# Norms and transpositions of x ahead of a data-dependent branch, in a fixed order, and bias rows loaded behind it

## The chip, the cores and the metric

The kernel runs on one core of one Trainium2 chip. A core has a matmul engine (TensorE, "PE" in the profile; its weight loads are "PEld"), VectorE ("DVE"), ScalarE ("ACT"), GpSimd ("POOL") and SyncE ("SP"), which here only issues DMAs. The engines run on their own and wait for each other by semaphores. The metric is the device time of the program in microseconds (us), as a median of several runs.

## The reference

A network of four graph layers over 512 nodes with 512 features. `src` and `dst` hold 16896 edges, sorted by `dst`, and `edge_type_2` gives each edge one of two types:

```python
h = max(layernorm(x), 0);  x = x + L0(h)   # dense attention, masked by the edges, 8 heads, then an MLP
h = max(layernorm(x), 0);  x = x + L1(h)   # two GIN layers: sum over edges, two products, batch norm
h = max(layernorm(x), 0);  x = x + L2(h)   # GCN: edges weighted by 1/sqrt(degree)
h = max(layernorm(x), 0);  x = x + L3(h)   # two relational layers, weights from 30 bases each
# L0, in the main:
q, k, v = h @ Wq + bq, h @ Wk + bk, h @ Wv + bv
scores = where(adj == 0, -1e9, q k^T / 8);  attn = softmax(scores, axis=1)
```

The change lies at the start: in the first layer norm, in what turns the edge lists into matrices of counts, and in the order of q, k and v.

## The kernel before

Everything has 128 rows (partitions), so x, 512 x 512, is four tiles, t = 0 to 3.

**Start.** SyncE loads the edge lists (`idx`) and x; then Wq, Wk and the first tiles of the basis matrices of layer 3 (the stream `bases`). GpSimd writes `lim` (the bounds that go with each chunk of edges), loads two small tables, writes the ramp `it` (an iota, L150) and, as the stream `rows` is made (L181), issues loads of the first four bias rows (L177). VectorE casts the edge lists to f32 (L390), TensorE transposes them (L392), and VectorE writes `key`: target, source and type of each edge, 128 edges to a chunk, 132 chunks.

**First norm.** `moments` (L342, L343) gives mean and variance of one tile of x. `first_norm` (L376) takes the square root on ScalarE (L378), the reciprocal and the scaled mean on VectorE (L379, L380), and writes h with ScalarE (L381). `flip` (L327) transposes one tile of h with four TensorE instructions into a PSUM bank (L331), and ScalarE copies it into `hT` (L335).

**Check for strays and branch.** The edges are sorted, so each chunk holds targets of a narrow range. `look_for_strays` (L406) compares every target with its bounds, reduces over the chunks on VectorE and over the partitions with a one-column matmul on TensorE (L414), and writes the result as `flag` (L418). All engines load the flag into a register (L460) and jump over `count_strays` if it is zero (L461), as it is for this input. Nothing that stands behind the branch in an engine's queue starts before.

**Counting, with the projections in between.** The matrices of edge counts are sums of one-hot products. For each chunk, `rows_of` (L538) makes two tiles: `hd` on VectorE (L543) and `hs`, for 75 of the 132 chunks on ScalarE (L547) and for the others on VectorE (L549). `count` (L552) multiplies the two with one matmul (L556); there are 204 counts in four blocks, which end at counts 49, 101, 153 and 203 (counted from 0), and rows are made up to 7 chunks ahead. When a block ends, `counted` (L559) empties its two PSUM banks with ScalarE and VectorE before the next block's counts can use them.

The projections of q, k and v (L478, L491) are generators that a plan (L698 to L719) advances between the counts: a "p" in the plan's string is half a projection of one tile, two f32 matmuls, which the profile shows as four records; after every second "p" a bias is added while the bank is copied out by ScalarE (L481). "G" is a basis step (L242), "s" and "S" are score blocks of the attention. FIRST is the number of the count behind which the plan begins, and the items are spread evenly from there to the end of the counting. `select` (L275) builds with 23 small VectorE operations the matrices that the basis steps need; it stands behind count 11. From there on all "p" use one PSUM bank.

**What sets the order.** The program is scheduled at build time: instructions that are not pinned may be moved by the scheduler, while those in `on(...)` (also passed as `keep`) stay in the order in which they are written, on their engine. Before the change the counts and rows up to count 10 were not pinned (`loose`), nor were `select`, the transpositions of h and two of the three ScalarE instructions that touch the norm.

**Behind it.** When the counting is over come the attention proper (VectorE), its products, the MLP and layers 1 to 3, mostly TensorE, which the change does not touch.

Of the kernel before, what the change touches and what calls it, by code (L numbers as in the profile page):

```python
# [74 lines left out]
def gnn_kernel(ctx: ExitStack, tc: tile.TileContext, out: bass.AP, a: dict):  # L75
# [102 lines left out]
            return t  # L178
        return load

    rows = Stream([row_load(i) for i in range(len(ROWS))], 4)  # L181

# [92 lines left out]
    def select():  # L275

        qi = rp.tile([P, NQ], I32, name="qi")
        nc.gpsimd.iota(qi, pattern=[[1, NQ]], base=0, channel_multiplier=0)
        q4 = rp.tile([P, NQ], F32, name="q4")
        nc.vector.tensor_copy(q4, qi)  # L280
        nb = FULL
        vi = rp.tile([P, nb], I32, name="vi")
        nc.gpsimd.iota(vi, pattern=[[-NQ, nb]], base=0, channel_multiplier=1)
        v = rp.tile([P, nb], F32, name="v")
        nc.vector.tensor_copy(v, vi)
        low = rp.tile([P, nb], F32, name="low")
        nc.vector.tensor_scalar(low, v, 0.0, None, op0=ALU.is_ge)
        sel = rp.tile([P, nb], F32, name="sel")
        nc.vector.scalar_tensor_tensor(sel, v, float(NQ - 1), low, op0=ALU.is_le, op1=ALU.mult)
        block = rp.tile([P, nb], F32, name="block")  # L290
        nc.vector.tensor_mul(block, v, sel)
        mine = rp.tile([P, 1], F32, name="mine")
        nc.vector.tensor_reduce(mine, block, AX.X, ALU.add)
        isq = rp.tile([P, NQ], F32, name="isq")
        nc.vector.tensor_scalar(isq, q4, mine, None, op0=ALU.is_equal)

        def fill(to, name, b0, b1, l, bases):

            at = AT1 + 2 * NB * l
            att = scal[:, at:at + 2 * NB].rearrange("p (x b) -> p x b", b=NB)[:, :, bases:bases + b1 - b0]  # L300
            pick = rp.tile([P, 2, b1 - b0], F32, name="pick" + name)
            nc.vector.tensor_mul(pick, att, sel[:, None, b0:b1].to_broadcast([P, 2, b1 - b0]))
            got = rp.tile([P, 2], F32, name="got" + name)
            nc.vector.tensor_reduce(got, pick, AX.X, ALU.add)
            for r in range(2):
                nc.vector.tensor_scalar(to[:, NQ * r:NQ * r + NQ], isq, got[:, r:r + 1], None, op0=ALU.mult)
# [13 lines left out]
    def ts(i):  # L320
        return slice(i * P, (i + 1) * P)

    def on(ins):

        return tc.keep_in_program_order(ins)

    def flip(src, s, dst=None):  # L327

        p = ps()
        for k in range(T):  # L330
            nc.tensor.transpose(p[:, ts(k)], src[:, s, ts(k)], ident)  # L331
# [37 lines left out]


    deg = const.tile([P, T], F32, name="deg")
    mv4 = rp.tile([P, T, 2], F32, name="mv4")
    by4 = rp.tile([P, T, 3], F32, name="by4")
    h = big("A")

    def first_norm(t):  # L376

        nc.scalar.activation(by4[:, t, 0:1], mv4[:, t, 1:2], AF.Sqrt, bias=eps)  # L378
        on(nc.vector.reciprocal(by4[:, t, 1:2], by4[:, t, 0:1]))  # L379
        on(nc.vector.tensor_scalar(by4[:, t, 2:3], mv4[:, t, 0:1], by4[:, t, 1:2], -1.0, op0=ALU.mult, op1=ALU.mult))  # L380
        nc.scalar.activation(h[:, t, :], x[:, t, :], AF.Relu, bias=by4[:, t, 2:3], scale=by4[:, t, 1:2])  # L381

    iot = ep.tile([P, N], F16, name="iot")
# [4 lines left out]
    kn = rp.tile([NCH // 2, 3, 2 * P], F32, name="kn")  # L388
    for i in range(3):
# [12 lines left out]
    stray = ep.tile([P, NCH], F32, name="stray")  # L402
    flag = const.tile([1, 1], I32, name="flag")
# [2 lines left out]
    def look_for_strays():  # L406
        over = rp.tile([P, NCH], F32, name="over")
        on(nc.vector.tensor_tensor(stray, key[:, 0, :], lim[:, 0, :], ALU.is_lt))
        on(nc.vector.tensor_tensor(over, key[:, 0, :], lim[:, 1, :], ALU.is_ge))
        on(nc.vector.tensor_add(stray, stray, over))  # L410
        some = rp.tile([P, 1], F32, name="some")
        on(nc.vector.tensor_reduce(some, stray, AX.X, ALU.max))
        p = ps()
        on(nc.tensor.matmul(p[0:1, 0:1], lhsT=some, rhs=ones, start=True, stop=True))  # L414
        on(nc.vector.tensor_copy(iot, it))
        on(nc.vector.tensor_scalar(key[:, 3, :], key[:, 1, :], -1.0, 0.5, op0=ALU.mult, op1=ALU.add))
        first_norm(2)
        on(nc.vector.tensor_copy(flag, p[0:1, 0:1]))  # L418
# [302 lines left out]
    loose = lambda ins: ins  # L721
# [479 lines left out]
```

## Time and profile before

| | us |
|---|---|
| median of three runs (519.61 to 520.34) | 519.86 |
| the profiled execution | 520.69 |
| its span in the profile | 518.4 |
| TensorE busy | 484.1 (93%) |
| VectorE busy | 399.8 (77%) |
| ScalarE busy | 195.5 (38%) |
| GpSimd busy | 38.1 (7%) |

Times in the profile count from the start of the span. "Busy" counts the time in which an engine executes something; a wait for a semaphore, and the issue of a DMA, are not busy time. In the timeline a row is: start, duration, engine, line of the code, operation, what is written and read, shape, "x" and how many instructions were merged, and in square brackets the idle time ahead of it and what ended that. Rows of one engine may overlap a little, since an engine starts an instruction before the last one's result is written. The chain of waits is the sequence of work that ended last, followed back from the last instruction. In the view by windows each engine has its busy time with the number of instructions in brackets, and behind them stand TensorE's granted clock (as a share of full), the share of busy DMA engines and GB/s.

### The profile page before, as it was taken

How to read it: one execution, taken by the hardware profiler on the slowest of the kernel's cores; microseconds unless marked ns; L12 is line 12 of the kernel's file. 1: busy time of each engine (PE TensorE's matmuls, PEld its weight loads, DVE VectorE, ACT ScalarE, POOL GpSimd, SP SyncE). 2: the span in 40 equal slices, each digit the busy share in tenths (PEclk: the TensorE clock that was granted, in tenths of full speed). 3: DMA queues.
4: the chain of work that ended last, by engine and by line, in shares of the span. 5: the costliest groups of instructions: out<-in, count | busy, mean ns of one | idle time of the engine just before them, and what ended most of it. 6: DMA issues, size and time to landing. Idle time of an engine off the chain costs nothing.

```text
span 518.4 us, 5734 instructions
## 1 busy us (share of the span) xinstructions
PE 484.1 (93%) x2014; PEld 248.6 (48%) x2014; DVE 399.8 (77%) x747; ACT 195.5 (38%) x318; POOL 38.1 (7%) x81
## 2 busy tenths in 40 slices
PE   2999999899998999999999994999799999999996
PEld 2333333345554538864545441644464484446642
DVE  6847587789999689999776982698549999998611
ACT  4876788625345113223321242124623610123000
POOL 7000000000000110300310000000010000000000
PEclk9999999999999999999999998999999999999999
DMA  7999778988968399495323759657972965520011
GB/s 250 272 242 259 175 191 192 248 223 187 224 161 188 92 242 297 169 270 215 117 107 131 184 152 292 236 135 190 272 181 88 316 185 207 192 87 3 0 42 40
DMA packets 42807, 94.06 MB, mean 181 GB/s; under 512 B 2097, under 2 KB 2295, under 8 KB 42775
## 3 DMA queue, kind: packets, MB, share of 16 engines
q1 hardware_dynamic: 34682, 68.30, 48.5%
q0 software_dynamic: 5712, 21.07, 13.7%
q10 hardware_dynamic: 2381, 4.26, 2.5%
q8 instruction: 20, 0.33, 0.3%
q14 instruction: 12, 0.10, 0.1%
HBM read 88.38 MB, written 5.24 MB: 181 GB/s over the span
## 4 chain that ended last, share of the span: by engine, by line
PE 65%; DVE 19%; ACT 9%; DMA 2%; issue 1%; ACTq 0%; DVEq 0%
PE pr L318 17%; PE acc L1109 11%; PE pg L318 9%; PE acc L1075 5%; PE ps L478 4%; PE bas L242 3%; DVE sc L642 3%; ACT sc L643 3%; ACT hs L547 3%; DVE sc L660 3%; DVE wrel L266 3%; PE ao L556 2%; PE acc L935 2%; DMA basis<-in_basis 2%; PE acc L318 2%; DVE half L636 2%
## 5 line engine op out<-in xcount | busy, mean ns | idle before, releaser
L266 DVE SCALAR_TENSOR_TENSOR wrel<-basis,scal,wrel 128x1024 f32<-128x1024 f32 x60 | 74.1, 1282 | 0.0
L242 PE MATMUL bas<-basis,wide 120*32 120x512 f32 (+1 forms) x320 | 44.6, 612 | 7.4 <-DMA basis<-in_basis 6.7
L547 ACT ACTIVATE hs<-iot,key 128x512 f16<-128x512 f16 x75 | 48.8, 711 | 4.7 <-PE ao L556 3.9
L543 DVE TENSOR_SCALAR hd<-iot,key 128x32 f16<-128x32 f16 (+1 forms) x132 | 33.3, 295 | 14.6 <-PE ao L556 14.3
L266 DVE SCALAR_TENSOR_TENSOR w<-basis,scal,w 128x1024 f32<-128x1024 f32 x32 | 39.4, 1283 | 0.0
L643 ACT ACTIVATE sc<-sc 128x2048 f32<-128x2048 f32 (+1 forms) x10 | 15.7, 1568 | 35.3 <-DVE sc L642 35.3
L556 PE MATMUL ao<-hs,hd 128*32 128x512 f16 x204 | 25.8, 396 | 2.8 <-ACT hs L547 2.6
L478 PE MATMUL ps<-bigB,w 128*128 128x512 f32 x56 | 27.2, 615 | 0.9 <-ACT bigD L481 0.6
L350 ACT ACTIVATE sd<-mv,eps 128x1 f32<-128x1 f32 x20 | 5.8, 295 | 43.5 <-DVE mv L343 42.4
L318 PE MATMUL pr<-bigE,w 128*128 128x512 f32 x48 | 21.4, 594 | 0.0
L1157 DVE TENSOR_TENSOR u<-acc,x 128x512 f32<-128x512 f32 x4 | 2.8, 692 | 23.5 <-PE acc L1109 23.5
L318 PE MATMUL pr<-bigD,w 128*128 128x256 f32 x88 | 20.2, 380 | 0.0
L549 DVE TENSOR_SCALAR hs<-iot,key 128x512 f16<-128x512 f16 x57 | 19.3, 347 | 0.0
L642 DVE TENSOR_TENSOR sc<-sc,half 128x2048 f32<-128x2048 f32 (+1 forms) x10 | 18.6, 1863 | 0.2
L242 PEld LDWEIGHTS bas<-basis,wide 120*32 120x32 f32 (+1 forms) x320 | 8.7, 109 | 20.9 <-issue 10.6
L660 DVE TENSOR_TENSOR sc<-sc,rec 128x2048 f32<-128x2048 f32 x8 | 18.3, 2285 | 0.0
L627 PE MATMUL psc<-bigC,bigD 64*128 64x256 f32 x128 | 18.1, 402 | 0.0
L318 PEld LDWEIGHTS pr<-bigD,w 128*128 128x128 f32 x88 | 16.6, 190 | 3.0 <-ACT bigE L880 0.8
L318 PE MATMUL pr<-w,bigE 128*128 128x512 f32 x40 | 17.8, 592 | 0.0
L556 PEld LDWEIGHTS <-hd 128*32 128x32 f16 x204 | 6.1, 94 | 23.8 <-issue 15.1
L478 PEld LDWEIGHTS ps<-bigB,w 128*128 128x128 f32 x56 | 9.7, 189 | 14.9 <-issue 11.1
L629 ACT COPY sc<-psc 128x1024 f32<-128x1024 f32 x16 | 15.6, 1006 | 2.6 <-issue 1.6
(314 smaller groups left out, 969.2 us busy)
## 6 DMA issues: line engine op xcount, KB each, us to landing
basis<-in_basis SPq DMA_DIRECT2D x32, 960.0 KB
basis<-in_basis SPq DMA_DIRECT2D x23, 1024.0 KB
basis<-in_basis SPq DMA_DIRECT2D x16, 448.0 KB
summed<-sums ACTq DMA_DIRECT2D x16, 256.0 KB
w<-in_W POOLq DMA_DIRECT2D x4, 1024.0 KB, 5.9
row<-in_rows POOLq DMA_DIRECT2D x12, 256.0 KB, 8.2
wrel<-summed POOLq DMA_DIRECT2D x4, 512.0 KB, 7.8
w<-in_conv_W1T POOLq DMA_DIRECT2D x2, 1024.0 KB, 5.8
```

The lines of the kernel that those rows point to most:

```text
L242: tc.keep_in_program_order(nc.tensor.matmul(sums[0][32 * j:32 * j + 32, :], lhsT=lhsT, rhs=t[:k, j, :], start=(g == 0), stop=(g == STEPS + ...
L266: on(nc.vector.scalar_tensor_tensor(to[r][:, i:i + 2, :], t[:, i:i + 2, :], scal[:, at:at + 1], to[r][:, i:i + 2, :], op0=ALU.mult, op1=AL ...
L318: nc.tensor.matmul(p, lhsT=lhsT, rhs=rhs, start=(i == 0), stop=(i == len(pairs) - 1))
L478: on(nc.tensor.matmul(p, lhsT=w[:, k, ts(m)], rhs=made["hT"][:, k, :], start=(k == 0), stop=(k == T - 1)))
L543: keep(nc.vector.tensor_scalar(hd[:, :w], iot[:, GW * groups_of[c][0]:GW * groups_of[c][0] + w], key[:, 0, c:c + 1], key[:, 2, c:c + 1], o ...
L547: keep(nc.scalar.activation(hs, iot, AF.Sign, bias=key[:, 3, c:c + 1]))
L556: keep(nc.tensor.matmul(cnt[b][GW * (g % T):GW * (g % T) + GW, :], lhsT=hd[:, at:at + GW], rhs=hs, start=(c == in_bank[g][b][0]), stop=(c ...
L642: on(nc.vector.tensor_sub(s, s, half[:, 0:1, :].to_broadcast([P, H // pieces, NH])))
L643: on(nc.scalar.activation(s, s, AF.Exp, scale=HD ** -0.5))
L660: on(nc.vector.tensor_mul(self.sc, self.sc, rec[:, None, :].to_broadcast([P, H, NH])))
L1075: nc.tensor.matmul(self.out[t], lhsT=self.hT[:, k, ts(t)], rhs=self.root[:, k, :], start=(k == 0), stop=False)
L1109: nc.tensor.matmul(self.out[t], lhsT=self.uT[r][:, k, ts(t)], rhs=wrel[r][:, k, :], start=False, stop=(r == 1 and k == T - 1))
```

## The change

Moments, norms and transpositions of all four tiles of x are written ahead of the check for strays, all pinned, with the square root taken out of `first_norm` so that it can stand earlier in ScalarE's order. Before, the moments and norm of tile 3 stood inside `look_for_strays`, behind the flag, tile 2's norm just ahead of it, and all four transpositions behind the branch in the text, though the scheduler put two of them ahead of it. The cast of the ramp (`iot`) moves ahead of the first moments, and the last part of `key` ahead of the check. The stream `rows` starts behind the branch, so the first four bias rows are issued by GpSimd there. `select`, and all rows and counts, are pinned, and FIRST is 4 in place of 9. No arithmetic is added or left out.

```diff
-    rows = Stream([row_load(i) for i in range(len(ROWS))], 4)
+    rows = Stream([row_load(i) for i in range(len(ROWS))], 0)
+    rows.ahead = 4
...
-        nc.vector.tensor_copy(q4, qi)
+        on(nc.vector.tensor_copy(q4, qi))
...
-    def flip(src, s, dst=None):
+    def flip(src, s, dst=None, keep=lambda ins: ins):
 
         p = ps()
         for k in range(T):
-            nc.tensor.transpose(p[:, ts(k)], src[:, s, ts(k)], ident)
+            keep(nc.tensor.transpose(p[:, ts(k)], src[:, s, ts(k)], ident))
...
-        nc.scalar.copy(dst[:, :, ts(s)], p)
+        keep(nc.scalar.copy(dst[:, :, ts(s)], p))
...
+    made = {"hT": big("B")}
...
+    def root(t):
+        on(nc.scalar.activation(by4[:, t, 0:1], mv4[:, t, 1:2], AF.Sqrt, bias=eps))
+
     def first_norm(t):
 
-        nc.scalar.activation(by4[:, t, 0:1], mv4[:, t, 1:2], AF.Sqrt, bias=eps)
         on(nc.vector.reciprocal(by4[:, t, 1:2], by4[:, t, 0:1]))
...
-        nc.scalar.activation(h[:, t, :], x[:, t, :], AF.Relu, bias=by4[:, t, 2:3], scale=by4[:, t, 1:2])
+        on(nc.scalar.activation(h[:, t, :], x[:, t, :], AF.Relu, bias=by4[:, t, 2:3], scale=by4[:, t, 1:2]))
...
+    on(nc.vector.tensor_copy(iot, it))
     moments(mv4[:, 0, :], x[:, 0, :], on)
     on(nc.vector.tensor_copy(key[:, 0:2, :], pk[:, 0:2, :]))
     on(nc.vector.tensor_scalar(key[:, 2, :], pk[:, 2, :], 0.0, LESS, op0=ALU.is_equal, op1=ALU.max))
 
+    root(0)
     moments(mv4[:, 1, :], x[:, 1, :], on)
-    for t in range(2):
-        first_norm(t)
+    first_norm(0)
+    root(1)
     moments(mv4[:, 2, :], x[:, 2, :], on)
+    root(2)
+    first_norm(1)
+    flip(h, 0, made["hT"], on)
+    moments(mv4[:, 3, :], x[:, 3, :], on)
+    root(3)
+    first_norm(2)
+    flip(h, 1, made["hT"], on)
+    first_norm(3)
+    for t in (2, 3):
+        flip(h, t, made["hT"], on)
+    on(nc.vector.tensor_scalar(key[:, 3, :], key[:, 1, :], -1.0, 0.5, op0=ALU.mult, op1=ALU.add))
...
         on(nc.tensor.matmul(p[0:1, 0:1], lhsT=some, rhs=ones, start=True, stop=True))
-        on(nc.vector.tensor_copy(iot, it))
-        on(nc.vector.tensor_scalar(key[:, 3, :], key[:, 1, :], -1.0, 0.5, op0=ALU.mult, op1=ALU.add))
-        first_norm(2)
         on(nc.vector.tensor_copy(flag, p[0:1, 0:1]))
-        moments(mv4[:, 3, :], x[:, 3, :], on)
-        first_norm(3)
...
     bases.start(AHEAD)
 
-    made = {}
-    made["h"], made["hT"] = h, big("B")
-    for t in range(T):
-        flip(made["h"], t, made["hT"])
+    rows.start(4)
+    made["h"] = h
...
-    FIRST = 9
+    FIRST = 4
...
-        keep = on if n > 10 else loose
...
-            rows_of(needed[made_rows], keep)
+            rows_of(needed[made_rows], on)
...
-        count(g, c, cnt, keep)
+        count(g, c, cnt, on)
```

The diff pins the other operations of `select` in the same way as the one shown.

More of the change, by code (lines that the diff above doesn't have):

```diff
@@ L284, in select @@
         v = rp.tile([P, nb], F32, name="v")
-        nc.vector.tensor_copy(v, vi)
+        on(nc.vector.tensor_copy(v, vi))
         low = rp.tile([P, nb], F32, name="low")
-        nc.vector.tensor_scalar(low, v, 0.0, None, op0=ALU.is_ge)
+        on(nc.vector.tensor_scalar(low, v, 0.0, None, op0=ALU.is_ge))
         sel = rp.tile([P, nb], F32, name="sel")
-        nc.vector.scalar_tensor_tensor(sel, v, float(NQ - 1), low, op0=ALU.is_le, op1=ALU.mult)
+        on(nc.vector.scalar_tensor_tensor(sel, v, float(NQ - 1), low, op0=ALU.is_le, op1=ALU.mult))
         block = rp.tile([P, nb], F32, name="block")
-        nc.vector.tensor_mul(block, v, sel)
+        on(nc.vector.tensor_mul(block, v, sel))
         mine = rp.tile([P, 1], F32, name="mine")
-        nc.vector.tensor_reduce(mine, block, AX.X, ALU.add)
+        on(nc.vector.tensor_reduce(mine, block, AX.X, ALU.add))
         isq = rp.tile([P, NQ], F32, name="isq")
-        nc.vector.tensor_scalar(isq, q4, mine, None, op0=ALU.is_equal)
+        on(nc.vector.tensor_scalar(isq, q4, mine, None, op0=ALU.is_equal))
         def fill(to, name, b0, b1, l, bases):
@@ L301, in fill @@
             pick = rp.tile([P, 2, b1 - b0], F32, name="pick" + name)
-            nc.vector.tensor_mul(pick, att, sel[:, None, b0:b1].to_broadcast([P, 2, b1 - b0]))
+            on(nc.vector.tensor_mul(pick, att, sel[:, None, b0:b1].to_broadcast([P, 2, b1 - b0])))
             got = rp.tile([P, 2], F32, name="got" + name)
-            nc.vector.tensor_reduce(got, pick, AX.X, ALU.add)
+            on(nc.vector.tensor_reduce(got, pick, AX.X, ALU.add))
             for r in range(2):
-                nc.vector.tensor_scalar(to[:, NQ * r:NQ * r + NQ], isq, got[:, r:r + 1], None, op0=ALU.mult)
+                on(nc.vector.tensor_scalar(to[:, NQ * r:NQ * r + NQ], isq, got[:, r:r + 1], None, op0=ALU.mult))
         for l in range(2):
@@ L374, in gnn_kernel @@
     h = big("A")
+    def root(t):
+        on(nc.scalar.activation(by4[:, t, 0:1], mv4[:, t, 1:2], AF.Sqrt, bias=eps))
     def first_norm(t):
-        nc.scalar.activation(by4[:, t, 0:1], mv4[:, t, 1:2], AF.Sqrt, bias=eps)
         on(nc.vector.reciprocal(by4[:, t, 1:2], by4[:, t, 0:1]))
         on(nc.vector.tensor_scalar(by4[:, t, 2:3], mv4[:, t, 0:1], by4[:, t, 1:2], -1.0, op0=ALU.mult, op1=ALU.mult))
-        nc.scalar.activation(h[:, t, :], x[:, t, :], AF.Relu, bias=by4[:, t, 2:3], scale=by4[:, t, 1:2])
-    iot = ep.tile([P, N], F16, name="iot")
+        on(nc.scalar.activation(h[:, t, :], x[:, t, :], AF.Relu, bias=by4[:, t, 2:3], scale=by4[:, t, 1:2]))
     key = ep.tile([P, 4, NCH], F32, name="key")
@@ L388, in gnn_kernel @@
     kn = rp.tile([NCH // 2, 3, 2 * P], F32, name="kn")
+    iot = ep.tile([P, N], F16, name="iot")
     for i in range(3):
@@ L719, in gnn_kernel @@
     plan.setdefault(len(order) - 14, []).append(lambda: blocks[0].pairs())
-    loose = lambda ins: ins
     made_rows = 0
     for n, (t, g, c) in enumerate(order):
-        keep = on if n > 10 else loose
         if n == 0 or order[n - 1][0] < t:
```

## The prediction

> **What bounds the kernel now.** I read the page first (TensorE is busy 93% of the span, and only the first of the 40 slices is thin, with 2 tenths), then the chain of waits, then the timeline of the first 35 us engine by engine, then single lines. The chain is unbroken work from 12.36 us on: count matmuls (L556) and projections (L478) on TensorE with ScalarE's rows and copies (L547, L481) in between up to 105 us, VectorE in the attention, TensorE again behind it. Nothing in it starts at a fixed time, and the DMA wait at 310.60 us (10.82 us) begins only when a buffer comes free. So a stage 1 that ends later moves the end by as much. The start of that chain:
>
> ```profile
> 12.49 1.10 PE ps L331 x4
> ...
> 15.58 1.11 PE psc L331 x4
> 16.69 1.15 PE ao L556 x7
> 17.84 2.54 PE psc L478 x4
> 20.37 0.33 PE ao L556 x4
> 20.70 1.91 PE psc L478 x4
> ```
>
> The columns are start and duration. Two of the four transpositions of h (L331) run behind the branch, then counts, and at 17.77 the first half projection ("p" in the plan: two f32 matmuls, four records) begins. It lasts 2.54 us, the next 1.91. The timeline shows what stands before it:
>
> ```profile
> 4.93 0.58 POOL L150 IOTA it<- 128x512 int32 x1
> ...
> 5.29 0.69 DVE L342 BATCH_NORM_STATS2 st<-x 128x6 f32<-128x512 f32 x1 [0.69 <-DMA x<-in_x]
> ...
> 7.87 1.52 ACT L381 ACTIVATE bigA<-x,by 128x512 f32<-128x512 f32 x2
> ...
> 10.94 0.14 DVE L418 CAST flag<-ps 1x1 int32<-1x1 f32 x1
> ...
> 12.44 0.18 DVE L343 BATCH_NORM_AGGREGATE mv<-st 128x2 f32<-128x6 f32 x1 [0.77 <-DVEq L461]
> ```
>
> The flag is ready at 11.08, VectorE goes on at 12.44 and TensorE at 12.46: the register load and branch cost 1.36 us.
>
> **Part 1: the flag comes later.** All four norms and transpositions now stand, in a fixed order, ahead of the flag's matmul (L414), on every engine. Durations and distances are those of the rows. VectorE: the cast of iot now precedes the first moments and needs the iota, done at 5.51; so it runs at 5.55 and the first statistics start at 5.88, not 5.29. Moments take 0.82 (6.63 to 7.45), the two key operations 0.51, the next moments 0.82, reciprocal and scaling 0.38: the first scale is ready at about 8.4. From there ScalarE, in its fixed order, is the limit: h0 8.45 (0.71 to the next), two square roots of 0.30, h1 at 9.91 (it waits 0.15 for its scale), copy of hT 10.62 (0.50), root, h2 11.42, copy 12.13, h3 12.63 to 13.44. TensorE's last four transpositions take 1.10 from 13.49 (8 took 1.97 at 8.73), and only then may the one-column matmul of 0.19 run: the flag is done at about **14.9**, 3.8 us later than now. VectorE's three new moments and the stray comparisons are done by 13.0 and hide beside that. With 1.36 us of branch VectorE starts the row tiles at 16.3. The unknown here is ScalarE's queue; 14.2 if the iota runs earlier, 15.7 if each hand-over costs 0.1 us more.
>
> **Part 2: the restart.** In exchange nothing but counting is left behind the branch. VectorE needs 0.22 us for each hd and 0.27 for each hs (ten hd in 2.21 us, three hs in 0.87); ScalarE's hs takes 0.66. The plan starts at count 4 rather than 9. The fifth count needs the hd of the fourth row, chunk 1: two hd and two hs, then two hd, 17.7, and the first half projection starts at about 17.85 against 17.77: **+0.1**. But only 5 counts are behind it, where the records before 17.77 show 11: 6 counts of 0.107 (5 in 0.54, at 42.30) are still to come, **+0.65**. Moving the start of the plan removes no work.
>
> **Part 3: TensorE's pace after a rest.** The granted-clock column says 1.00 for the first 20 us, but the same transposition tells otherwise:
>
> ```profile
> L331 PE MATMUL pr<-ident,bigA x24: 272/273/273, 247.5 to 461.1; 128*128 128x128 f32 x24
> ...
> L331 PE MATMUL psc<-ident,bigA x12: 421/421/477, 8.7 to 16.3; 128*128 128x128 f32 x12
> ```
>
> It takes 421 ns up to 16.3 us and 273 later, and the first half projection lost 2.54 - 1.91 = 0.63 us. Half pace for the first 1.26 us of it explains this: full pace from about 19.1, 3.5 us after TensorE became busy without a break (15.58). The one other rest is seen with its clock:
>
> ```profile
> 310.00:320.00 10.00, 4.08 (x32) 1.02 (x30) 3.75 (x13) 4.12 (x7) 0.75 (x1) 0.97 0.85 222
> 320.00:325.00 5.00, 3.54 (x14) 1.78 (x15) 0.00 (x0) 0.52 (x1) 0.00 (x0) 0.50 1.04 390
> 325.00:330.00 5.00, 5.00 (x21) 4.03 (x21) 4.88 (x5) 0.66 (x2) 0.00 (x0) 0.87 1.04 386
> ```
>
> (The column after the last "(x..)" is the granted clock.) Work resumed at 321.46, eight basis matmuls took 1.94 us where 0.86 is usual, and 0.87 in the next window means 1.3 us more of half pace: to 326.3, 4.8 us after the restart. So a restart costs 3.5 to 4.8 us of half pace. After the change the transpositions ahead of the branch have gaps (each waits for its h), then TensorE rests from 14.8 to 17.0, and dense work begins at about 17.4: full pace at 20.9 to 22.2. Half of the time since 17.85 is lost, 1.5 to 2.2, less the 0.63 lost now: +0.9 to +1.5, I take **+1.2**. From below: if those transpositions already bring full pace, nothing is lost and the 0.63 is won back.
>
> [...]
>
> **Part 4: select in one piece.** Its 23 small VectorE operations (0.17 to 0.23 each; 18.10 to 22.1 now, with four hs among them, so 2.9 net) are now pinned at count 11: dependent ones are 0.2 apart, 3.7 us in one block from about 22.2 to 25.9. Queued behind it is the hd of chunk 22, which count 21 needs. With that hd done at 26.2 and Part 3's pace, TensorE gets there at about 27 (three half projections and 16 counts after 17.85), so the block is covered: **0**. Without Part 3's loss it gets there at 25.4 and waits 0.8.
>
> **Part 5: the first row end.** At count 49 the next block's counts need the banks that ScalarE and VectorE empty. Now two half projections (3.70 us from 34.67) cover that, and counts resume at 38.38; after, one half projection and a basis step, 1.91 + 0.86 = 2.77, cover a release that takes 2.9 to 3.7: +0.1 to +0.9, less what ScalarE gains by having copied the previous projection earlier; I take **+0.3**, bounds 0 and 0.8. The basis step itself is only moved (from count 57).
>
> **Costed at nothing.** The four bias-row issues on GpSimd (2.15 us) go behind the branch: there they delay the iotas and memsets of select to about 18.7, which VectorE needs at 22.2; uncovered they would cost what exceeds 3.5 us. Their first reader (L494) comes after 69 us. Their absence early lets x land sooner, which gains nothing since the iota ends the first wait. SP's queue passes the branch 3.8 us later, with two basis loads and Wv: the third basis tile is wanted past 54 us and Wv at 67.61, against 13.1 us for the slowest landing of a weight that the DMA view shows in the first 40 us (Wo), and requests already queued keep the DMA engines busy meanwhile (share 1.02 from 10 to 20). Uncovered, at most those 3.8 us. Pinned rows and counts up to count 10 add no instruction.
>
> **Sum:** 0.1 + 0.65 + 1.2 + 0 + 0.3 = **+2.2 us**. The profiled execution took 520.69 us (span 518.4, 2.29 around it), so about 522.9 for it; it lies 0.83 above the median of the three runs, so that I state **522.0** for the median, 519.86 + 2.2 rounded. The forecast's own range: from +0.9 (full pace, 0.63 won back, select's 0.8 showing: 0.1 + 0.65 - 0.63 + 0.8) to +4.0 (flag 0.8 later, 1.5, 0.8): 520.8 to 523.9.
>
> **Rivals.** *No change that can be told:* the transpositions ahead of the branch wake TensorE, and the select block and the row end are covered: 0.1 + 0.65 - 0.63 = +0.1, 520.0. For it: there TensorE is busy some 4.4 of 5.3 us. Against it: now it is busy 3.4 of the 4.2 us from 12.49 to 16.69, partly with counts, and the first projection is slow still.
>
> *Faster:* the hand-back of the one projection bank. Weight loads of L478 wait 1.3 us in all for ScalarE's copies into bigC and 2.1 for those into bigD. If the shifted plan removed all of it, -3.4 + 2.2 = -1.2, 518.7; it decides once more than 3.2 us of those waits go. Against it: the plan leaves 4, 3, 7, 9, 4, 4, 5 counts between a copy and the next projection now, and 4, 4, 3, 7, 4, 4, 8 after; hardly different.
>
> That the order isn't obeyed is unlikely, since all those instructions are pinned.
>
> **How the numbers follow.** Forecast 0.70, no change 0.20, faster 0.10. A measurement can tell 0.2%, 1.04 us, from nothing: faster means under 518.82, slower over 520.90. Nearly all of the forecast lies above it (0.68), with 0.02 falling to "same": 0.10, 0.22, 0.68. The range reaches down past the no-change case to 519.7 and up to 523.7; what is left out is the faster case and the tail of a late flag with a long half pace.
>
> **What would show it.** The flag at 14.2 to 15.7, VectorE's first hd about 1.4 us behind it, the first L478 at 17.4 to 18.6 lasting 3 us or more, select in one block of 3.5 us or more, counts resuming 2.9 us or more after the 50th. Wrong: a first half projection of 1.9 us; a flag before 13; or a shift at 35 us that is gone at 105, which would mean that stage 1 has slack that I don't see.

## The result and the profile after

| us | before | after |
|---|---|---|
| median (range) of four runs each, same chip | 520.10 (519.61 to 522.06) | 528.31 (527.71 to 530.00) |
| profiled execution, its span | 520.69, 518.4 | 530.00, 528.1 |
| TensorE, VectorE, ScalarE busy | 484.1, 399.8, 195.5 | 488.5, 404.2, 195.3 |

After over before is 1.0156, with a 95% interval of 1.0120 to 1.0191: **8.2 us slower** by the medians, where +2.2 was predicted. A second set of runs (e9 below) gave 1.0164 [1.0140, 1.0188]. The sign was right and the size was not.

It arises in stage 1. From the first matmul of the attention's sums (line 654 in before, 664 in after) to the end the two profiles differ by 1.1 us only, and that has a cause of its own (below). The table cuts stage 1 at points that every kernel here has: the flag's end, the starts of the first four half projections (p0 to p3), and that first matmul of the sums. The columns with "to" are distances.

| us | flag | p0 | p0 to p1 | p1 to p2 | p2 to p3 | p3 to sums | sums at |
|---|---|---|---|---|---|---|---|
| before | 11.08 | 17.77 | 2.86 | 2.46 | 2.46 | 75.97 | 101.52 |
| after | 18.23 | 21.46 | 4.63 | 2.45 | 3.26 | 78.31 | 110.11 |
| after less before | +7.15 | +3.69 | +1.77 | 0 | +0.80 | +2.34 | +8.59 |

The prediction's terms for the same cuts were +0.1 (p0), +1.2 (p0 to p1), 0 (p2 to p3) and +0.95 (the counts deferred, 0.65, and the row end, 0.3, both behind p3). Every cut is above its term, the first by most. The timeline of after shows why the flag is late (columns as before: start, duration, engine, line, operation, in brackets the idle time ahead and what ended it):

```profile
2.75 3.45 POOL L144 TENSOR_SCALAR lim<-lim 128x66 f32<-128x66 f32 x3
3.36 2.99 DVE L394 CAST kn<-idx 66x256 f32<-66x256 int32 x3 [2.46 <-DMA idx<-in_dst]
...
6.68 0.58 POOL L150 IOTA it<- 128x512 int32 x1
...
7.29 2.15 DVE L397 CAST iot<-it 128x512 f16<-128x512 int32 x1 [0.94 <-POOL it L150]
7.33 1.82 POOL L471 MEMSET apart<- 128x2048 bf16 x1
9.08 2.15 POOL L177 DMA_DIRECT2D row<-in_rows  x4
...
18.08 0.15 DVE L432 CAST flag<-psc 1x1 int32<-1x1 f32 x1 [1.57 <-PE psc L431]
...
21.46 3.78 PE L488 MATMUL psc<-bigB,w 128*128 128x512 f32 x4
```

The same operations in the timeline of before:

```profile
2.75 1.71 POOL L144 TENSOR_SCALAR lim<-lim 128x66 f32<-128x66 f32 x3
3.26 1.34 DVE L390 CAST kn<-idx 66x256 f32<-66x256 int32 x3 [2.36 <-DMA idx<-in_dst]
...
7.72 1.82 POOL L459 MEMSET apart<- 128x2048 bf16 x1
...
10.09 0.42 DVE L415 CAST iot<-it 128x512 f16<-128x512 int32 x1
```

The cast of `iot` took 0.42 us before, at 10.09, when GpSimd was idle. Here it lies beside GpSimd's memset of `apart`, which keeps its usual 1.82, and takes 2.15, ending 0.29 behind the memset. The three casts of `kn` took 1.34 before and take 2.99 here. The first of them alone, and GpSimd's third addition, from the timeline around 3.8 us:

```profile
3.36 2.51 DVE L394 CAST kn<-idx 66x256 f32<-66x256 int32 x1 [2.46 <-DMA idx<-in_dst]
...
3.46 2.73 POOL L144 TENSOR_SCALAR lim<-lim 128x66 f32<-128x66 f32 x1
```

The cast takes 2.51 us where the two behind it take 0.31 each, and the addition 2.73 where the same one took 0.99 in before. This also pushes GpSimd's iota from 4.93 to 6.68 and so the cast of `iot` behind it. The row at 9.08 says another thing: GpSimd issues the four bias rows there, ahead of the branch, although they are written behind it, since they are not pinned.

The chain of waits of after, start and duration, shows the rest of the loss:

```profile
20.05 1.48 PE ao L566 x5
21.53 3.71 PE psc L488 x4
...
175.98 4.54 PE ps L664 x12
```

and at the same place in the chain of before:

```profile
167.41 2.86 PE ps L654 x12
```

Five counts in 1.48 us and a first half projection of 3.71 (2.54 before): TensorE at half pace. The first record of the granted clock in each trace, full pace, stands at 19.1 us in before and at 26.0 here; ahead of it the clock's column in the view by windows shows 1.00, and the half pace is seen in the durations alone. The 12 matmuls at 175.98 account for what is lost behind stage 1. By the clock's records TensorE is at half pace from 176.2 to 179.6, behind a wait that both kernels have. A timeline row and a window of after (the clock is the third number from the end):

```profile
175.98 1.93 PE L664 MATMUL ps<-z,ident 128*128 128x256 f32 x4 [1.78 <-DVE z L658]
```

```profile
175.00:180.00 5.00, 4.02 (x11) 3.26 (x12) 2.89 (x2) 1.96 (x3) 0.00 (x0) 0.66 0.97 205
```

The profile of e9, the same kernel once more, does not have it (2.86 for the 12).

### The profile page after: what moved, and what is told of

It is laid out like the page before. It is cut to its first block, busy times and chain, and to the rows that moved or that the text cites. A ratio compares the mean times of both kernels' runs of the same rounds, so it can differ in the third digit from the quotient of the medians.

```text
span 528.1 us, 5737 instructions
## 1 busy us (share of the span) xinstructions
PE 488.5 (93%) x2014; PEld 249.8 (47%) x2014; DVE 404.2 (77%) x747; ACT 195.3 (37%) x318; POOL 39.5 (7%) x81
## 4 chain that ended last, share of the span: by engine, by line
PE 63%; DVE 19%; ACT 9%; DMA 3%; issue 2%; ACTq 0%; DVEq 0%
PE pr L319 17%; PE acc L1116 10%; PE pg L319 9%; PE acc L1082 5%; PE ps L488 4%; PE bas L243 3%; DVE sc L652 3%; ACT sc L653 3%; DVE wrel L267 2%; ACT hs L557 2%; PE acc L942 2%; DVE sc L670 2%; DMA basis<-in_basis 2%; PE ao L566 2%; PE acc L319 2%
## 5 line engine op out<-in xcount | busy, mean ns | idle before, releaser
L653 ACT ACTIVATE sc<-sc 128x2048 f32<-128x2048 f32 (+1 forms) x10 | 15.7, 1570 | 35.6 <-DVE sc L652 28.6
L501 PE MATMUL ps<-w,bigB 128*128 128x512 f32 x32 | 15.9, 618 | 1.0 <-DVE bigE L504 1.0
```

Of the source, the lines that this page charges most:

```text
L653: on(nc.scalar.activation(s, s, AF.Exp, scale=HD ** -0.5))
```

## The experiments

The profiled positions of the runs that are compared by them, cut as above. Medians and ratios stand with each run; before had 519.87, 520.58, 520.56 and 520.62 in the four sets (7, 11, 16 and 27 runs).

| us | kn, iot casts | flag | p0 | p0 to p1 | p2 to p3 | p3 to sums | sums at |
|---|---|---|---|---|---|---|---|
| e1 | 3.05, 0.42 | 15.15 | 18.38 | 4.45 | 3.42 | 78.29 | 106.99 |
| e2 | 3.10, 0.44 | 12.00 | 19.42 | 4.68 | 3.19 | 78.29 | 108.05 |
| e3 | 1.26, 2.15 | 16.35 | 19.62 | 4.40 | 2.45 | 78.29 | 107.22 |
| e4 | 4.44, 0.41 | 17.23 | 21.97 | 3.94 | 2.45 | 75.90 | 106.72 |
| e5 | 3.05, 0.42 | 15.13 | 19.95 | 3.48 | 2.46 | 75.90 | 104.24 |
| e6 | 1.21, 0.43 | 14.78 | 18.02 | 3.96 | 3.42 | 78.30 | 106.15 |
| e7 | 2.98, 0.42 | 14.69 | 18.33 | 2.45 | 3.42 | 78.31 | 104.96 |
| e9 | 3.14, 2.15 | 18.23 | 21.46 | 3.61 | 3.42 | 78.30 | 109.25 |
| e13 | 0.89, 0.42 | 14.19 | 17.42 | 4.00 | 3.42 | 78.29 | 105.58 |
| e14 | 1.05, 0.42 | 13.64 | 18.46 | 4.48 | 2.46 | 75.90 | 103.76 |
| e15 | 1.28, 0.42 | 10.65 | 17.34 | (p0 to p2 5.57) | 2.45 | 78.29 | 103.65 |
| e16 | 1.27, 0.42 | 11.06 | 17.75 | 3.66 | 2.46 | 75.96 | 102.28 |

Two columns take only two values each. p3 to sums is 78.3 in every kernel whose plan begins at count 4 and 75.9 to 76.0 in every one that begins at count 9. p2 to p3 is 3.2 to 3.4 only where that plan, the pinned `select` and the pinned first rows and counts are together.

### First set: one part of the change taken back

**e1, the cast of `iot` back ahead of the flag's copy**

```diff
-    on(nc.vector.tensor_copy(iot, it))
     moments(mv4[:, 0, :], x[:, 0, :], on)
...
+        on(nc.vector.tensor_copy(iot, it))
         on(nc.vector.tensor_copy(flag, p[0:1, 0:1]))
```

> After the change, with the cast of iot moved back behind the reduction of the strays; all else stays. Theory A (the flag is late, and of its 7.1 us some 3.3 come from two VectorE casts that GpSimd's work beside them stretches: kn 0.86 to 2.51, iot 0.42 to 2.15): the cast's wait of 0.6 and its stretch of 1.7 leave the path to the flag, which comes at 14.3 to 16.0; 2.3 us less than the changed kernel, about 526. Rival B (what was lost lies behind the branch, in the plan that starts at count 4 and in the pinned counts; the flag's delay is covered): less than 0.5 us of change.

525.99, ratio 1.0109 [1.0088, 1.0131]. The flag comes 3.08 us earlier than in after, the time falls by 2.3.

**e2, norms and transpositions as before; rows, `select` and plan as changed**

```diff
-    for t in (2, 3):
-        flip(h, t, made["hT"], on)
...
+    made["h"], made["hT"] = h, big("B")
+    for t in range(T):
+        flip(made["h"], t, made["hT"])
```

> After the change, with the block of moments, norms and transpositions as it was before the change (tiles 2 and 3 around the flag, two transpositions behind the branch, iot and the last part of key inside the check); select, rows and counts stay pinned and the plan begins at count 4. Theory A: the flag comes at 11 to 12.7 and 5 to 7.5 us are won back, 521 to 523. Rival B: within 1.5 us of the changed kernel, 527 or more.

526.59, ratio 1.0106 [1.0074, 1.0137]. The flag is back at 12.00, and yet p0 starts at 19.42: with the rows pinned behind the transpositions' copies in ScalarE's order, the first `hs` starts at 17.52 where before it started at 14.10. Undoing the largest suspect alone gains 1.7 us, between the two times expected, because the pinned queue takes over what the flag no longer costs.

**e3, `select` not pinned**

```diff
-        on(nc.vector.tensor_copy(q4, qi))
+        nc.vector.tensor_copy(q4, qi)
```

> After the change, with select's 23 VectorE operations not pinned. Theory A: the count that waits 0.4 us for VectorE's hd at 31.48 and the pinned block in front of it cost 0.8, so 527.5. Rival C (the block is covered by TensorE's half pace, as predicted): no change, 528.3. Rival B says nothing of it.

526.15, ratio 1.0105 [1.0056, 1.0154]. p2 to p3 falls from 3.26 to 2.45, with no wait of a count for VectorE. In this profile the flag is also 1.88 earlier, since the casts of `kn` were not stretched.

**e4, the plan at count 9 and the first counts not pinned**

```diff
-    FIRST = 4
+    FIRST = 9
...
+        keep = on if n > 10 else loose
-            rows_of(needed[made_rows], on)
+            rows_of(needed[made_rows], keep)
```

> After the change, with FIRST back at 9 and rows and counts up to count 10 not pinned. Theory A: 0 to 1 us less (the row end at count 49 is covered by two half projections again), 527.3 to 528.3. Rival B: 4 us less or more, 524 or under.

525.83, ratio 1.0102 [1.0075, 1.0128]. p3 to sums is 75.90, as before. All four are 1.0% over the kernel before, and no single part explains the 1.6%.

### Second set: parts alone, and the two suspects of the start

**e5, norms and transpositions alone** (e1, e3 and e4 together)

> The kernel before with the norms and transpositions of all of x ahead of the flag alone: iot is cast late, select is not pinned, rows and counts are as before with the plan from count 9 (the bias rows stay where the change puts them). Theory A2 (three costs that partly stand in for each other: the late flag, the pinned queue behind the branch, select in one block): the part that I predicted, without the stretched casts and the block, is left; flag at 14.3 to 16, 1.5 to 3 us over the kernel before, 521.5 to 523. Rival D (pinning costs most, the norm block by itself little): within 1 us of before.

523.03, ratio 1.0051 [1.0035, 1.0068], at the upper end of what was expected.

**e6, after with GpSimd's memset held back until `key` is written**

```diff
-    nc.gpsimd.memset(apart, 1.0)
+    late = rp.tile([1, 1], F32, name="late")
+    on(nc.gpsimd.tensor_copy(late, key[0:1, 0, 0:1]))
+    on(nc.gpsimd.memset(apart, 1.0))
```

> The changed kernel, with GpSimd's memset of apart made to wait for key, so that it can't run beside the cast of iot. The order on VectorE is unchanged. If the cast is stretched by the memset beside it: 0.42 us in place of 2.15, flag 1.7 earlier than in the changed kernel, time 1.7 less, 526.6. If the cast is slow because of its place or of the DMAs that land then: 2.15 still, no change.

524.21, ratio 1.0068 [1.0052, 1.0083]. Rows of its timeline:

```profile
3.39 1.21 DVE L394 CAST kn<-idx 66x256 f32<-66x256 int32 x3 [2.49 <-DMA idx<-in_dst]
...
5.55 0.43 DVE L397 CAST iot<-it 128x512 f16<-128x512 int32 x1 [0.95 <-POOL it L150]
...
7.33 1.79 POOL L473 MEMSET apart<- 128x2048 bf16 x1
...
14.64 0.14 DVE L432 CAST flag<-psc 1x1 int32<-1x1 f32 x1 [1.57 <-PE psc L431]
...
18.02 3.49 PE L490 MATMUL psc<-bigB,w 128*128 128x512 f32 x4
```

VectorE's work and order are those of after. On GpSimd the memset stands behind three of the bias rows' issues, and in this profile the casts of `kn` are not stretched, so that the iota and the cast of `iot` come earlier. The cast takes 0.43 at 5.55 and the flag is there at 14.78: the prediction's 5.55 and 14.9. e3 has unstretched casts of `kn` too, but the memset beside the cast of `iot`:

```profile
3.01 1.26 DVE L394 CAST kn<-idx 66x256 f32<-66x256 int32 x3 [2.11 <-DMA idx<-in_dst]
...
5.41 2.15 DVE L397 CAST iot<-it 128x512 f16<-128x512 int32 x1 [1.13 <-POOL it L150]
5.44 1.82 POOL L471 MEMSET apart<- 128x2048 bf16 x1
```

So the work ahead of the flag was rightly summed; what was missing is what GpSimd does beside it. The time fell by 4.1 us by the medians where 1.7 was expected; the unstretched casts of `kn` would account for much of that, but why they are so here is not known.

**e7, e1 with TensorE kept busy ahead of the branch** (16 matmuls of zeros, whose result is not used)

```diff
+    def wake(n):
+        for _ in range(n):
+            on(nc.tensor.matmul(cnt_first[0], lhsT=zero, rhs=zero[:, 0:1].to_broadcast([P, 512]), start=True, stop=True))
...
         on(nc.tensor.matmul(p[0:1, 0:1], lhsT=some, rhs=ones, start=True, stop=True))
+        wake(14)
```

> The changed kernel with iot cast late, and 16 matmuls on zeros added on TensorE (one behind each of the first two transpositions, 14 behind the flag's matmul), whose result is not used. If TensorE's rest ahead of the counts costs half pace: the first half projection takes 1.9 to 2.6 us in place of 3.7, and the time is 1 to 1.5 less than with iot late alone (525.99), 524.7. If the 3.7 us are a wait for something else: 3.7 still, no gain, up to 0.5 slower.

524.46, ratio 1.0072 [1.0054, 1.0090]. TensorE's rows in its timeline:

```profile
14.44 3.22 PE L398 MATMUL ao<-zero 128*128 128x512 f16 x14
...
18.33 1.98 PE L498 MATMUL psc<-bigB,w 128*128 128x512 f32 x4
...
20.78 1.98 PE L498 MATMUL psc<-bigB,w 128*128 128x512 f32 x4
```

With full pace from 13.0 us p0 takes 1.98, p0 to p1 is 2.45 in place of 4.45, and the sums come 2.03 earlier than in e1 (1.5 by the medians). The slow start is the clock's, not a wait for data.

**e8, before, with GpSimd's additions held back behind the casts of `kn`**

```diff
-    for t in range(1, T):
-        nc.gpsimd.tensor_scalar_add(over_tiles[:, :, t, :], over_tiles[:, :, t, :], float(P * t))
...
+    late = rp.tile([1, 1], F32, name="late")
+    on(nc.gpsimd.tensor_copy(late, kn[0:1, 2, 0:1]))
+    for t in range(1, T):
+        on(nc.gpsimd.tensor_scalar_add(over_tiles[:, :, t, :], over_tiles[:, :, t, :], float(P * t)))
...
-    nc.gpsimd.memset(apart, 1.0)
+    on(nc.gpsimd.memset(apart, 1.0))
```

> The kernel before, with GpSimd's three additions to lim made to wait until the casts of kn are done. Four of six profiles so far show these casts at 3.0 to 4.4 us in all, two at 1.3. If that is work of both engines side by side: 1.3 us always, no run of the kernel near 521.3, and the median 0.5 to 1.5 under before, 518.5 to 519.4. If the casts wait for their DMA: 3.0 or more in some profiles, no change.

524.64, ratio 1.0074 [1.0046, 1.0103], for another reason than the one tried: GpSimd, free of the additions, issued the bias rows at 3.94 instead of 5.59, the third tile of x landed late (VectorE idle 2.90 us at 10.75, ended by the load of x), and the flag came at 13.60. The order of the issues on GpSimd does matter here, in the direction opposite to the change's.

### Third set: a repeat, and attempts at a faster kernel

**e9, after once more**

> The changed kernel once more, beside runs of the kernel before on the same chip. Theory A2: iot's cast is stretched to some 2.1 us again in the profile (the memset of apart always starts beside it) and the time is 3 us or more over e6 (524.2), 527 to 528.5. If the stretch was chance: 0.42 us, 524 to 525.

529.08, ratio 1.0164 [1.0140, 1.0188]. Both casts stretched as in the first profile, 3.14 and 2.15.

**e10, before with additions, `scal` and bias rows all behind the casts of `kn`**

```diff
...
-    rows = Stream([row_load(i) for i in range(len(ROWS))], 4)
+    rows = Stream([row_load(i) for i in range(len(ROWS))], 0)
+    rows.ahead = 4
...
+    on(nc.gpsimd.memset(apart, 1.0))
...
+    rows.start(4)
```

The additions and the load of `scal` move as the additions do in e8.

> The kernel before, with GpSimd's additions to lim behind the casts of kn, the small table scal behind these, and the bias rows behind the memset of apart, so that nothing large is loaded beside x (e8 loaded the rows 1.65 us earlier, and the third tile of x came 2.9 us late). kn 1.2 to 1.3 us in the profile; if the stretch of kn is what spreads the runs of the kernel before (519.6 to 522), all runs lie near its lowest: median 0.5 to 1 less. If not: no change.

520.75, ratio 1.0003 [0.9991, 1.0015]. Casts of 0.69, flag at 11.06: nothing gained, nothing lost.

**e11, before with e7's matmuls of zeros; e12, e10 and e11 together** (the results of those matmuls are not used)

```diff
+    wake(13)
     for t in range(2):
         first_norm(t)
+    for t in range(2):
+        flip(h, t, made["hT"], on)
...
+        wake(6)
```

> The kernel before, with 19 matmuls on zeros on TensorE ahead of the branch (13 behind the edge lists' transpositions, 6 behind the flag's matmul), the first two transpositions pinned. The half pace costs the kernel before at least 0.63 us in the first half projection and some 0.4 in the counts ahead of it: 0.6 to 1.2 us less than before. Rival: TensorE isn't what the first projection waits for, no change.

> Both of the two last in one kernel: 1 to 2 us less than the kernel before if they add up.

524.48, ratio 1.0082 [1.0059, 1.0105], and 525.14, ratio 1.0092 [1.0076, 1.0107]. TensorE in e11:

```profile
10.78 0.60 PE L331 MATMUL ps<-ident,bigA 128*128 128x128 f32 x4
...
15.71 0.63 PE L331 MATMUL ps<-ident,bigA 128*128 128x128 f32 x4 [2.36 <-DVEq L473]
...
19.91 3.78 PE L489 MATMUL psc<-bigB,w 128*128 128x512 f32 x4
```

The transpositions run at twice the pace (four in 0.60, 1.1 before), but the branch still leaves TensorE 2.36 us idle, and the clock falls back to half from 17.6 to 24.4, over p0, which takes 3.78 in place of 2.60. The flag is 1.04 later too, at 12.12. Here the early work did not help, since the pace that it won was lost again behind the branch: of the 3.41 us up to 17.6 TensorE was busy for 1.39. No kernel of the study beats the one before.

### Fourth set: what each part costs with the casts undisturbed

**e13, after with GpSimd's additions, `scal` and memset held back behind the cast of `iot`**

```diff
...
     on(nc.vector.tensor_copy(iot, it))
+    late = rp.tile([1, 1], F16, name="late")
+    on(nc.gpsimd.tensor_copy(late, iot[0:1, 0:1]))
+    for t in range(1, T):
+        on(nc.gpsimd.tensor_scalar_add(over_tiles[:, :, t, :], over_tiles[:, :, t, :], float(P * t)))
+    nc.gpsimd.dma_start(scal, a["scal"].to_broadcast([P, NSC]))
...
-    nc.gpsimd.memset(apart, 1.0)
+    on(nc.gpsimd.memset(apart, 1.0))
```

VectorE's order is that of after, in which the cast of `iot` already stands right behind those of `kn`; it runs earlier because GpSimd, without the additions, has the iota done earlier. The load of `scal` is not pinned and was issued ahead of the additions, at 3.38.

> The changed kernel with GpSimd kept quiet while VectorE makes its casts: the cast of iot moved straight behind the three of kn, and behind it, in this order, GpSimd's three additions on lim, the load of scal and, behind the flag's work, the memset of apart. Nothing is left out. Theory (both stretched casts are paid in nearly every run of the changed kernel): kn's casts 0.7 to 1.3 us and iot's 0.43, the flag at 13.9 to 14.9, and the time is the changed kernel's 529.1 less 1.7 for iot and 1.7 for kn and what hangs on them, 522.3 to 523.5. Rival (the stretch of kn is an accident of single profiles and most runs of the kernel before have it too): as with the memset alone held back, 524.2. Rival (a late flag isn't what the time hangs on): above 526.

524.37, ratio 1.0084 [1.0067, 1.0101]. From its timeline:

```profile
3.15 0.89 DVE L391 CAST kn<-idx 66x256 f32<-66x256 int32 x3 [2.25 <-DMA idx<-in_dst]
...
3.96 0.42 DVE L394 CAST iot<-it 128x512 f16<-128x512 int32 x1
...
4.65 1.09 POOL L398 TENSOR_SCALAR lim<-lim 128x66 f32<-128x66 f32 x3
...
14.04 0.15 DVE L434 CAST flag<-psc 1x1 int32<-1x1 f32 x1 [1.57 <-PE psc L433]
...
17.42 3.54 PE L490 MATMUL psc<-bigB,w 128*128 128x512 f32 x4
...
26.97 0.39 PE L568 MATMUL ao<-hs,hd 128*32 128x512 f16 x1 [0.57 <-DVE hd L555]
```

Neither cast is stretched, and p0 starts at 17.42, earlier than in before. The sums come 4.53 us earlier than in after's profile, and the median is 4.7 below e9's. The expected 522.3 to 523.5 was wrong: the time is e6's (524.2), which was the rival's number. The rival's reason, that most runs of the kernel before have stretched casts of `kn` too, is not shown; e6's profile has unstretched ones, which explains the equal times as well.

**e14, e5 with the casts undisturbed in the way of e10**

> Norms and transpositions ahead of the check alone (iot late, select unpinned, the plan at count 9), with GpSimd's additions, the load of scal and the memset of apart held back behind kn's casts. Theory (kn's stretch is part of what the norm block alone cost in its run, 2.45 us): the flag near 13.5, first half projection near 18.3, 521.0 to 521.8 against 520.6. Rival (the stretch isn't in most runs, and the block costs that by its half pace and ScalarE's queue): 523.0 as before.

521.79, ratio 1.0032 [1.0015, 1.0050]. Between the two expectations, and its interval overlaps e5's [1.0035, 1.0068]: likely part of e5's time was the stretch of `kn`, but this is not shown.

**e15, before with the plan at count 4 alone**

```diff
-    FIRST = 9
+    FIRST = 4
```

> The kernel before with one edit: the plan starts at count 4, not at 9. Theory (the term of 0.65 us for counts deferred, and 1.4 us at the row end of count 153, where the second score block moves behind its counts): the two score blocks of that place 4.4 us apart instead of 3.0, the first half projection within 0.2 us of 17.77, and 522.0 to 522.7 against 520.6. Rival (counts deferred fill waits that stand later in stage 1): 520.6 within 0.5, stage 1 ending within 0.5 us of 101.5.

523.27, ratio 1.0053 [1.0034, 1.0073], a little above what was expected. The start is 0.43 us earlier in this profile, p0 6.69 behind the flag as in before. p0 to p3 is 8.02 against 7.78, p3 to sums 78.29 against 75.97. Of the 2.3 us between these two, 1.4 lie where two score blocks (L621) stand close together. TensorE there in before, then in e15:

```profile
77.83 0.60 PE L621 MATMUL psc<-apart,far_off 128*128 128x512 bf16 x2
...
79.43 0.64 PE L556 MATMUL ao<-hs,hd 128*32 128x512 f16 x6
80.31 0.59 PE L556 MATMUL ao<-hs,hd 128*32 128x512 f16 x2 [0.24 <-ACT hs L547]
80.83 0.61 PE L621 MATMUL psc<-apart,far_off 128*128 128x512 bf16 x2
```

```profile
78.56 0.60 PE L621 MATMUL psc<-apart,far_off 128*128 128x512 bf16 x2
...
81.22 0.39 PE L556 MATMUL ao<-hs,hd 128*32 128x512 f16 x2 [0.45 <-ACT hs L547]
81.83 0.38 PE L556 MATMUL ao<-hs,hd 128*32 128x512 f16 x1 [0.22 <-ACT hs L547]
82.44 0.59 PE L556 MATMUL ao<-hs,hd 128*32 128x512 f16 x2 [0.24 <-ACT hs L547]
82.97 0.60 PE L621 MATMUL psc<-apart,far_off 128*128 128x512 bf16 x2
```

4.41 us from one block to the next in place of 3.00 (4.40 in after and e13). Two more counts stand between them, and counts wait for `hs` three times (0.91 in all) instead of once (0.24). ScalarE, which makes `hs`, is late there: its timeline in e15 shows

```profile
79.50 1.06 ACT L643 ACTIVATE sc<-sc 128x1024 f32<-128x1024 f32 x1 [0.33 <-DVE sc L642]
80.46 1.93 ACT L547 ACTIVATE hs<-iot,key 128x512 f16<-128x512 f16 x3
```

The attention's exponential (L643) waits for VectorE and stands in ScalarE's order ahead of the rows that TensorE needs next.

**e16, before with `select` pinned alone**

> The kernel before with one edit: select's VectorE operations pinned in one block at count 11. Theory (VectorE is close to what TensorE waits for there): the block 3.5 to 4.3 us long, one wait of TensorE for a hd ahead of the third half projection or the fourth, 0.8 to 1.2 us on stage 1, 521.4 to 521.8 against 520.6. Rival (covered, as the prediction had it): no wait, 520.6 within 0.4.

520.81, ratio 1.0005 [0.9991, 1.0018]. The block is 4.16 us long (19.14 to 23.30), and TensorE does not wait for it:

```profile
23.86 1.98 PE L478 MATMUL ps<-bigB,w 128*128 128x512 f32 x4
25.77 0.61 PE L556 MATMUL ao<-hs,hd 128*32 128x512 f16 x6
26.32 1.99 PE L478 MATMUL ps<-bigB,w 128*128 128x512 f32 x4
```

Alone it is covered, as predicted, and the theory of the expectation was wrong.

**The sum.** By the ratios times 520.6, the parts alone cost 1.7 (e14, norms and transpositions), 2.8 (e15, the plan) and 0.3 us (e16, `select`), together 4.7; the three together without stretched casts cost 4.4 [3.5, 5.3] (e13). The change as it is costs 8.5 [7.3, 9.8] (e9). What remains, some 4.1, goes with the two casts: the flags of e9 and e13 are 4.04 apart. The pinning of the first rows and counts was not run alone; in e13 it is included.

## Why the prediction was right in sign and wrong in size

In the profile of after, stage 1 ends some 6.3 us later than the prediction's terms had it. 3.3 of these are the flag, 1.4 lie behind p3, 0.8 are a wait behind `select`, 0.6 the slow start and 0.3 the restart.

**Part 1, the flag: the failed step.** The prediction took the cast of `iot` at its duration of before ("so it runs at 5.55 and the first statistics start at 5.88") and allowed only for an earlier iota and for hand-overs (14.2 to 15.7). It moved the cast from a place where GpSimd was idle to one beside GpSimd's memset. Measured: 2.15 in place of 0.42, and a flag at 18.23. With neither cast stretched (e6) the flag is at 14.78, with that of `iot` alone stretched (e3) at 16.35. So of the 3.45 us from 14.78 to 18.23 the memset beside `iot` costs 1.57. The other 1.88 come with the casts of `kn`, which the change does not touch, by way of GpSimd's addition and iota beside them (the iota at 6.68 in place of 4.93).

That the `iot` stretch is the memset's is shown: it is there in after, e9 and e3 (2.15 each), where the two overlap, and gone wherever they don't (0.41 to 0.44), in e6 at nearly the same time as in e3. For `kn` less is certain. It was 2.98 to 3.14 in six profiles of the changed kernel and its variants, 4.44 in e4 (its third cast alone lasts from 3.90 to 7.40, long past the additions, and ends 0.15 behind the memset of `apart`), but 1.21 to 1.26 in e3 and e6, 1.27 to 1.34 in before, e15 and e16, whose start is the same code, and 1.02 in e11. Additions and casts overlap in all of these. In the six, the first cast ends at 5.86 to 5.88 wherever it had started (3.21 to 3.37). What decides, and why the kernels that carry the change fall on the long side more often, stays open, and so does its share of the 4.1 us.

**The branch** costs what was said: from the flag to VectorE's first operation behind the branch 1.41 us (1.36 predicted).

**Part 2, the restart.** p0 came 3.23 us behind the flag, 2.95 predicted. The 0.65 for deferred counts was right in kind: with this plan 22 counts stand ahead of p3 in place of 27 (after, e13, e15), and the other five, at 0.107 each, are in p3 to sums.

**Part 3, half pace: right in kind, its size partly by luck.** +1.2 was predicted for the slow start; from p0 to p1 it measured +1.14 in e13 and +1.77 in after, and e7 takes it away. But e9, the same kernel as after with p0 at the same 21.46, has +0.75, with full pace from 23.8 in place of 26.0. The kernel before had a short one in its profile: e10 and e16 start p0 within 0.02 us of it, but reach full pace at 20.3 and 20.6 in place of 19.1, and take 3.48 and 3.66 from p0 to p1 in place of 2.86. So this term is uncertain by some 1 us. That is also why the parts' profiles don't simply add: e14's flag is 1.49 us earlier than e5's, its p0 to p1 1.00 longer, and its full pace comes at 22.7, later than e5's 22.1.

The clock's records show how long half pace lasted inside the two runs: 6.83 us in before (319.42 to 326.25), 3.41 and 6.83 in after (176.16 to 179.58 and 329.76 to 336.59).

**Part 4, `select`: 0 was right alone and wrong in company.** The text had the block from 22.2 to 25.9 and TensorE at 27. In e13, where the flag is near its forecast, the block is longer, 4.17 in place of 3.7 (22.45 to 26.62), and TensorE is there earlier, at 26.40: it waits 0.57 for the `hd` behind the block. In e16 the same block starts at 19.14; there 11 counts stand ahead of p0, in e13 five, and counts free the rows' buffers. So the pinning of `select` alone did not use up the cover. The plan's shift or the pinning of the first rows did; no run separates these two. The 0.8 kept as the bound is about the size that came (0.80 to 0.96).

**Part 5 and the plan: mis-sized.** The first row end gave nothing (0.3 predicted): in before and after TensorE waits 0.20 there for VectorE. The 2.3 us came elsewhere, 0.5 from the counts deferred and 1.4 from the third row end (the rest stays open), where the prediction called the two plans "hardly different" after comparing only the counts between copies and projections. It did not walk the shifted plan through ScalarE's order at the score blocks.

**Costed at nothing.** The bias rows did not go behind the branch, though they are written there: they were issued at 9.08, and `select`'s iotas right behind them, from 11.23, so nothing was delayed.

**The range.** Its upper end was put at +4.0, but the terms named for it add up to 3.85; what came lies far outside both.

**The rivals.** No change would have needed full pace at p0, which none but e7 had. The faster one would have needed fewer waits for the projection bank; p3 to sums is longer by 2.3 in every kernel with this plan.

## What to carry to other kernels

When an operation is moved, look at what the other engines do at its new place, and take its duration only from a row with the same neighbours: here a 0.42 us cast became 2.15 beside a memset. When a plan that interleaves engines is shifted by a few steps, walk it to its end on every engine: the loss came 60 us later, where one engine's queue order met the shifted steps. A part that is free alone may cost once another part has used its cover, so measure parts alone and together. Before a difference of 1 or 2 us between two profiles is put down to an edit, compare where the clock changes in both: here the same rows gave 3.61 and 4.63 from p0 to p1.

## What was not expected of the hardware

- A VectorE cast took longer beside GpSimd's work, and GpSimd's work beside a cast. int32 to f16, 128x512: 0.42 in before, with GpSimd idle, and 2.15 in after, beside a memset of 1.82; the cast started 0.04 ahead of the memset and ended 0.29 behind it. int32 to f32, 66x256: 0.28 in e13 (the third cast, at 3.76, with only the issue of a load on GpSimd) and 2.51 in after, beside an addition that itself took 2.73, where the two additions ahead of it took 0.44 and 0.41. The f32 statistics of VectorE were not stretched beside the same additions (in e13 0.69 at 4.91, the usual time, with the additions from 4.65 to 5.74). By what the two engines hold each other up in these cases no run shows.
- Half pace came back long after the start: in after at 176.16, 150.19 us after full pace had begun. It cost 12 matmuls 1.7 us (4.54 in place of the 2.86 of before and e9); in e2 and e3 they took 4.54 as well, from 173.94 and 173.09. Of e9's six runs, the three at 526.93 to 528.07 have a mean granted clock of 0.992 or 0.993 and the three at 530.10 to 530.37 one of 0.990: a spread as large as most parts of this change are worth.
- The clock's changes in before (19.05, 319.42, 326.25, 517.40) and in after (25.98, 176.16, 179.58, 329.76, 336.59, 527.74) lie whole multiples of 3.413 us apart within each trace: 88, 90 and 146 of them from the first in before, 44, 45, 89, 91 and 147 in after. In the 3.41 us ahead of a change from full to half TensorE was busy for 0.00 (319.42) and 0.12 (517.40) in before, 1.63 (176.16), 0.00 (329.76) and 0.00 (527.74) in after. Ahead of 169.24 in before, 44 multiples from its first change, it was busy for 1.82, the least there behind which full pace stayed. Ahead of every change from half to full it was busy throughout (3.41); halfway through the two stretches of 6.83, behind 1.38 (322.84 in before) and 1.87 (333.18 in after), half pace stayed. How much work keeps or wins full pace is not shown closer than by these figures, and the point from which the multiples count is not the kernel's start: after and e9 have the same rows up to p0 at 21.46 and reach full pace at 26.0 and 23.8.
